# Attention score rows of 576 keys in one PSUM tile of two banks, a running minimum of negated scores, and small operations moved off VectorE

## The chip, the cores and the metric

The kernel runs on one core of a Trainium2 chip. Its engines are TensorE (PE in the profile; its weight loads are PEld), VectorE (DVE), ScalarE (ACT), GpSimd (POOL) and SyncE (SP), which issues most of the DMAs. A time is the device time of the whole program in microseconds (us); the lower the better. Before the change three runs took 1487.26, 1487.73 and 1488.32 us: median 1487.73.

## The reference

One transformer layer over a sequence of 2048 tokens of width 256, all in float32: differential attention, then a feed-forward block, each behind a layernorm, followed by a layernorm and a residual addition. Cut to what matters here:

```python
qkv = hidden @ Wqkv_w.T + Wqkv_b              # 16 query heads, 8 key heads of 128
s  = (q_m . k_m) * 128**-0.5, causal          # m = 0, 1: the two maps of a pair
p  = softmax(s_0) - lam * softmax(s_1)        # 8 pairs of heads in 4 groups
o  = p @ v                                    # v: 4 groups of width 256
o  = o * rsqrt(mean(o*o) + 1e-5) * subln_w * (1 - LAMBDA_INIT)
x  = x + layernorm(o @ out_w.T + out_b)
x  = x + layernorm(ffn(layernorm(x)))         # two Hadamard transforms, silu gate
```

`lam` comes from four small vectors. Every score row is divided by its own sum of exponentials, and the row's maximum is taken off before the exponential.

## The kernel before

**Units and steps.** The attention goes through 4 groups; a group has its 2 query pairs side by side, so 64 queries of both pairs fill the 128 partitions. A block of 128 tokens (`i` = 0 to 15) has two halves of 64 queries. For `i` < 8 one *unit* covers both halves, above that each half is a unit of its own: 24 units in a group, 96 in all. A half `s` of block `i` sees L = 128 i + 64 (s + 1) keys. Group 0 goes up through the blocks; groups 1 to 3 take the long ones first, downwards, then the short ones, downwards.

The order of every engine's instructions is written out by hand: a loop over steps calls the parts of several units in turn, and dictionaries (`before`, `mid`, `between`, `after`) put projections, weight loads and pieces of the feed-forward at given steps. Each engine runs its own instructions in that order; waits are set from the tiles that are read and written. In step s:

- `begin`, `scores(new, 0)`: score matmuls of the first half of the unit's score rows (each row once for each of the two maps m), into PSUM tiles of two banks (`sc`, pool `ps_s`, three buffers, which projections, transposes and the feed-forward use as well). [...] VectorE copies the scores into `e` and keeps a running maximum in `mx` (L270); the last 64 keys get the causal mask and end the maximum in `last` (L281). A small VectorE operation makes the bias `nb` = -SCALE x last (L293).
- `exponentials` (ScalarE, L298): Exp with bias `nb` and scale SCALE, in place, with the row's sum in `d`.
- `inverse` of the unit of step s - 4: VectorE forms `u` = ss/256 + ed (L395), GpSimd its power -0.5 `f` (L399), and GpSimd scales the unit's output rows `osb` by it (L401). `ss` is the sum of squares of the output row, `ed` = EPS x d x d.
- `turn_out` of the unit of step s - 5, where its block is complete: VectorE transposes `osb` into `xo` (L417), and SP writes it out and reads it back transposed (`oT`).
- `combine` of the unit of step s - 1 on VectorE: reciprocal of the second sum (L317), `cf` (L319), e0 + cf x e1 (L325), then 32x32 transposes (L347), a DMA to DRAM and four back (`pt`, by SP); last of all `ed` (L333).
- Then projections put there, `scores(new, 1)`, `values` of the unit of step s - 3 (TensorE into `po`; ScalarE copies it to `osb` and squares it with a sum into `ss`, L382 and L385), `project_out`, and `exponentials(new, 1)`.

**Cutting rows into tiles.** A row has up to 1024 columns in one tile. Rows of 576, 1088 and 1600 keys are cut by hand:

```python
if L % 512 == 64 and L > 64:
    first = 320 if L == 576 else 704
    return [first, L - first]
```

So a row of 576 keys takes two tiles, with 320 and 256 columns. There are two such rows (m = 0 and 1) in each group, both in the unit `i` = 4.

**Start.** The projections (L174) are evicted by ScalarE and VectorE with a bias column of `colv` (L192, L194); `colv` is loaded by a DMA of GpSimd. `load_lambdas` issues four more loads on GpSimd's queue, and 16 columns of `colv` hold the biases of the query heads. The last stage, from about 1310 us on, is the feed-forward alone; pieces of it already run beside the last units.

## Time and profile before

| | |
|---|---|
| median of three runs | 1487.73 us |
| profiled execution, its own time | 1489.19 us |
| its span | 1487.4 us |
| TensorE busy | 1458.2 us (98%) |
| VectorE busy | 1080.8 us (73%) |
| ScalarE busy | 498.6 us (34%) |
| GpSimd busy | 287.1 us (19%) |
| score matmuls (L260), 1280 records | 481.3 us |
| score scans (L270), two groups | 231.5 and 100.5 us |
| masked last scan (L281), 248 records | 70.4 us |

The profile is one execution, recorded by the hardware. Busy time is the time in which an engine has an instruction at work; matmuls overlap each other, so a busy TensorE is not one at its peak. A float32 matmul shows as two records (two passes). In lists of waits, "A <- B" means that A stood until B had ended. In lists of groups, the columns are line, engine, operation, output<-inputs, shapes, count | busy us, mean ns of one | idle time before it and what ended most of it. In a timeline the columns are start (us), duration (us), engine, line, operation, count, and in brackets the idle time before it. Line numbers are those of the kernel before.

### The profile page before, as it was taken

The numbers are of one execution on the slowest core, as the hardware profiler recorded it, in microseconds if no ns is written. First come the engines' busy times: TensorE is split into PE (matmuls) and PEld (weight loads), VectorE is DVE, ScalarE is ACT, GpSimd is POOL, SyncE is SP. The second block draws the span as 40 slices with busy tenths as digits, with TensorE's granted clock in tenths as the row PEclk, the third lists the DMA queues.
The fourth block names the chain that finished last, engine by engine and source line by source line (L and its number), as shares of the span: only waits on it lengthen the run. The fifth ranks groups of instructions, "written<-read, shape, count | busy, mean of one in ns | idle before, by whom it ended". The sixth has DMA issues, their size and how long they took to land.

```text
span 1487.4 us, 17643 instructions
## 1 busy us (share of the span) xinstructions
PE 1458.2 (98%) x5488; PEld 1040.3 (70%) x5488; DVE 1080.8 (73%) x2828; ACT 498.6 (34%) x1011; POOL 287.1 (19%) x379
## 2 busy tenths in 40 slices
PE   8899999999999999999999999999999999999998
PEld 5567777656766776665677776665776666888887
DVE  4489788847666889654878787547898888866674
ACT  2354334333123334322423334324223334541211
POOL 2022222101111121110321211112221221322110
PEclk9999999999999999999999999999999999999999
DMA  3049898866467787721898788424987768522000
GB/s 116 21 107 188 184 193 186 152 121 128 88 141 147 168 201 166 149 78 43 183 171 189 164 198 176 98 64 91 252 181 160 161 154 172 137 79 64 26 25 15
DMA packets 463838, 198.41 MB, mean 133 GB/s; under 512 B 366177, under 2 KB 460913, under 8 KB 463745
## 3 DMA queue, kind: packets, MB, share of 16 engines
q1 hardware_dynamic: 459616, 187.36, 58.8%
q0 software_dynamic: 2592, 8.48, 2.0%
q10 hardware_dynamic: 1536, 1.44, 0.3%
q8 instruction: 45, 0.74, 0.2%
q14 instruction: 49, 0.39, 0.1%
HBM read 104.95 MB, written 92.27 MB: 133 GB/s over the span
## 4 chain that ended last, share of the span: by engine, by line
PE 86%; DVE 11%; DMA 1%; issue 1%; ACT 1%; ACTq 0%; SPq 0%; POOL 0%; POOLq 0%; DVEq 0%
PE po L371 28%; PE sc L260 25%; PE pp L174 11%; PE gu L650 7%; PE pout L438 7%; PE pd L680 4%; PE pv L202 4%; DVE e L270 3%; DVE e L325 2%; DVE e L347 2%; DVE e L281 1%; DMA wq<-in_wqkvT 1%; DVE xo L417 0%; PE tx L637 0%; DVE nb L293 0%
## 5 line engine op out<-in xcount | busy, mean ns | idle before, releaser
L260 PE MATMUL sc<-k,q 128*128 128x512 f32 (+7 forms) x1280 | 481.3, 522 | 14.6 <-DVE last L281 8.9
L371 PE MATMUL po<-v,pt 128*128 128x256 f32 x2176 | 485.4, 379 | 0.0
L371 PEld LDWEIGHTS po<-v,pt 128*128 128x128 f32 x2176 | 425.3, 196 | 57.6 <-issue 10.2
L260 PEld LDWEIGHTS sc<-k,q 128*128 128x128 f32 x1280 | 236.7, 191 | 238.5 <-issue 188.3
L298 ACT ACTIVATE e<-e,nb 128x192 f32<-128x192 f32 (+28 forms) x256 | 299.4, 1170 | 296.9 <-DVE u L395 172.6
L270 DVE TENSOR_SCALAR_CACHE_REDUCE e<-sc 128x1024 f32<-128x1024 f32 (+14 forms) x248 | 231.5, 934 | 158.3 <-PE sc L260 157.7
L399 POOL TENSOR_TENSOR f<-u,mhalf 128x1 f32<-128x1 f32 (+1 forms) x96 | 59.5, 620 | 948.2 <-DVE u L395 644.6
L382 ACT COPY osb<-po 128x256 f32<-128x256 f32 (+1 forms) x96 | 42.7, 444 | 427.1 <-PE po L371 427.0
L174 PE MATMUL pp<-xnT,wq 128*128 128x512 f32 x384 | 173.7, 603 | 3.8 <-ACT xnT L498 2.4
L347 DVE STREAM_TRANSPOSE e<-e 128x768 f32<-128x768 f32 (+7 forms) x192 | 172.4, 938 | 6.7
L401 POOL TENSOR_SCALAR osb<-osb,f 128x256 f32<-128x256 f32 x128 | 172.3, 1351 | 9.5
L325 DVE SCALAR_TENSOR_TENSOR e<-e,cf,e 128x64 f32<-128x64 f32 (+31 forms) x128 | 170.6, 1353 | 3.4
L174 PEld LDWEIGHTS pp<-xnT,wq 128*128 128x128 f32 x384 | 73.4, 193 | 88.8 <-issue 80.5
L438 PE MATMUL pout<-wo,oT 128*128 128x256 f32 x512 | 120.9, 379 | 0.0
L270 DVE TENSOR_SCALAR_CACHE_REDUCE e<-sc,mx 128x192 f32<-128x192 f32 (+13 forms) x136 | 100.5, 739 | 23.6 <-PE sc L260 9.5
L438 PEld LDWEIGHTS pout<-wo,oT 128*128 128x128 f32 x512 | 97.3, 190 | 12.8
L281 DVE CUSTOM_DVE_ANT_0 e<-sc,mask,mx 128x64 f32<-128x64 f32 x248 | 70.4, 284 | 8.9
L663 ACT ACTIVATE hT<-gu,colv 128x256 f32<-128x256 f32 x64 | 30.4, 475 | 133.6 <-PE gu L650 89.6
L650 PE MATMUL gu<-fxnT,wgate 128*128 128x256 f32 x256 | 65.8, 379 | 0.2 <-DVE last L281 0.2
L650 PE MATMUL gu<-fxnT,wup 128*128 128x256 f32 x256 | 65.7, 379 | 0.0
L664 DVE SCALAR_TENSOR_TENSOR hT<-gu,colv,hT 128x256 f32<-128x256 f32 x64 | 30.9, 482 | 40.1 <-ACT hT L663 40.0
L202 PE MATMUL pv<-wq,xnT 128*128 128x256 f32 x256 | 57.6, 380 | 0.9 <-DVE xnT L499 0.8
(105 smaller groups left out, 942.6 us busy)
## 6 DMA issues: line engine op xcount, KB each, us to landing
dr<-e SPq DMA_DIRECT2D x20, 1024.0 KB, 4.7
pt<-dr SPq DMA_DIRECT2D x80, 256.0 KB, 5.8
dr<-e SPq DMA_DIRECT2D x20, 896.0 KB, 4.3
pt<-dr SPq DMA_DIRECT2D x80, 224.0 KB, 5.1
do<-xo SPq DMA_DIRECT2D x64, 256.0 KB, 3.0
oT<-do SPq DMA_DIRECT2D x256, 64.0 KB, 2.8
dr<-e SPq DMA_DIRECT2D x20, 768.0 KB, 4.0
pt<-dr SPq DMA_DIRECT2D x80, 192.0 KB, 4.5
```

The costliest lines, as they stand in the source:

```text
L174: nc.tensor.matmul(pp[:, ts(h, 512)], lhsT=wq[:, c, ts(j, P)], rhs=xnT[:, c, cols4], start=(c == 0), stop=(c == 1),)
L202: nc.tensor.matmul(pp[:, ts(t, 256)], lhsT=xnT[:, c, ts(nb * 4 + t, P)], rhs=wq[:, c, 768:1024], start=(c == 0), stop=(c == 1),)
L260: nc.tensor.matmul(sc[:, lo : lo + ww], lhsT=qT[m][:, u.i, u.subs[a]].rearrange("d p q -> d (p q)"), rhs=kT[m][:, at + lo : at + lo + ww], ...
L270: nc.vector.tensor_scalar(e[:, at : at + full], sc[:, :full], 1.0, best, ALU.mult, ALU.max, accum_out=u.mx[:, k0, c : c + 1],)
L281: nc.vector.tensor_tensor_reduce(e[:, L - 64 : L], sc[:, full : full + 64], mask, 1.0, best, ALU.add, ALU.max, accum_out=u.last[:, k0 : k0 ...
L298: nc.scalar.activation(e, e, AF.Exp, bias=u.nb[:, 2 * a + m : 2 * a + m + 1], scale=SCALE, accum_out=u.d[:, a, m : m + 1],)
L325: nc.vector.scalar_tensor_tensor(e0, e1, cf[:, a : a + 1], e0, ALU.mult, ALU.add)
L347: nc.vector.transpose(xv[:, r], ev[:, r])
L371: nc.tensor.matmul(u.po[:, ts(a, HID)], lhsT=ptv[:, g, r, :], rhs=vt[:, kc, :], start=(kc == 0), stop=(kc == u.i),)
L401: nc.gpsimd.tensor_scalar(u.osb[:, a, :], u.osb[:, a, :], f[:, a : a + 1], None, ALU.mult)
L438: nc.tensor.matmul(u.pout[:, :HID], lhsT=u.oT[:, c, p, :], rhs=wos[u.g][:, p, c, :], start=(p == 0 and c == 0), stop=(p == 1 and c == 1),)
L650: nc.tensor.matmul(ps[:, ts(2 * j + n, 256)], lhsT=ffn[which][:, c, ts(fc, P)], rhs=xnT[:, c, :], start=(c == 0), stop=(c == 1),)
```

## The change

Six edits, all in the attention:

1. A row of 576 keys takes one tile: 256 columns in its first bank, 320 in the second. One VectorE scan reads the 512 unmasked ones out of both banks, the masked one reads the 64 at column 768. Rows of 1088 and 1600 keys are cut as before.
2. The queries are projected as -SCALE x q: the evictions get a scale, and the 16 bias columns of the query heads are multiplied by -SCALE once, on GpSimd, ahead of the loads in `load_lambdas`. Scores are then negated and scaled, the running maximum becomes a running minimum, mask and start value change sign, and Exp takes `last` as its bias with scale -1. `nb` and its operation are gone.
3. `ed` is made by ScalarE (Square with a scale, 256 EPS d d) behind the Exps of the unit's second half, in place of VectorE at the end of `combine`.
4. `u` is an addition on GpSimd, ss + ed, in place of VectorE.
5. The factor 16 that is then missing in `f` is a second scalar in GpSimd's scaling of `osb`.
6. The query evictions of VectorE become a multiplication and an addition in one operation.

```diff
@@ project_heads
+                scale = -SCALE if j < 4 else 1.0
                 if h == 0 or not both:
-                    nc.scalar.activation(dst, src, AF.Identity, bias=bias)
+                    nc.scalar.activation(dst, src, AF.Identity, bias=bias, scale=scale)
                 else:
-                    nc.vector.tensor_scalar(dst, src, bias, None, ALU.add)
+                    nc.vector.tensor_scalar(dst, src, scale, bias, ALU.mult, ALU.add)
...
         def cuts(L):
 
-            if L % 512 == 64 and L > 64:
-                first = 320 if L == 576 else 704
-                return [first, L - first]
+            if L == 1088 or L == 1600:
+                return [704, L - 704]
             return [min(1024, L - c) for c in range(0, L, 1024)]
...
-            u.nb = sm.tile([P, 4], F32, tag="nb", name=f"nb_{u.n}")
...
-                best = LOWEST
+                best = HIGHEST
...
-                    for lo in range(0, w, 512):
-                        ww = min(512, w - lo)
+
+                    step = 256 if w == 576 else 512
+                    los = [0, 256] if w == 576 else range(0, w, 512)
+                    for k, lo in enumerate(los):
+                        ww = w - lo if k == len(los) - 1 else step
                         nc.tensor.matmul(
-                            sc[:, lo : lo + ww],
+                            sc[:, 512 * k : 512 * k + ww],
...
+                    tail = 768 if w == 576 else full
                     if full:
+                        dst, src = e[:, at : at + full], sc[:, :full]
+                        if w == 576:
+                            dst = dst.rearrange("p (k c) -> p k c", k=2)
+                            src = sc.rearrange("p (k c) -> p k c", k=2)[:, :, :256]
                         nc.vector.tensor_scalar(
-                            e[:, at : at + full],
-                            sc[:, :full],
+                            dst,
+                            src,
                             1.0,
                             best,
                             ALU.mult,
-                            ALU.max,
+                            ALU.min,
                             accum_out=u.mx[:, k0, c : c + 1],
                         )
...
-                            sc[:, full : full + 64],
+                            sc[:, tail : tail + 64],
                             mask,
                             1.0,
                             best,
                             ALU.add,
-                            ALU.max,
+                            ALU.min,
                             accum_out=u.last[:, k0 : k0 + 1],
                         )
                     at += w
-            lo, hi = (2 * half, 2 * half + 2) if u.ns == 2 else (half, half + 1)
-            nc.vector.tensor_scalar(u.nb[:, lo:hi], u.last[:, lo:hi], -SCALE, None, ALU.mult)
...
                     AF.Exp,
-                    bias=u.nb[:, 2 * a + m : 2 * a + m + 1],
-                    scale=SCALE,
+                    bias=u.last[:, 2 * a + m : 2 * a + m + 1],
+                    scale=-1.0,
                     accum_out=u.d[:, a, m : m + 1],
+                )
+            if half:
+
+                u.ed = sm.tile([P, 2], F32, tag="ed", name=f"ed_{u.n}", bufs=8)
+                nc.scalar.activation(
+                    u.ed[:, : u.ns], u.d[:, : u.ns, 0], AF.Square, scale=16.0 * math.sqrt(EPS)
                 )
@@ combine
-            u.ed = sm.tile([P, 2], F32, tag="ed", name=f"ed_{u.n}", bufs=8)
...
-            nc.vector.scalar_tensor_tensor(
-                u.ed[:, : u.ns], d1, EPS, d1, ALU.mult, ALU.mult
-            )
@@ inverse
-            nc.vector.scalar_tensor_tensor(
-                w[:, : u.ns], u.ss[:, : u.ns], 1.0 / 256.0, u.ed[:, : u.ns], ALU.mult, ALU.add
-            )
+            nc.gpsimd.tensor_tensor(w[:, : u.ns], u.ss[:, : u.ns], u.ed[:, : u.ns], ALU.add)
             nc.gpsimd.tensor_tensor(f[:, : u.ns], w[:, : u.ns], mhalf[:, : u.ns], ALU.pow)
             for a in range(u.ns):
                 nc.gpsimd.tensor_scalar(
-                    u.osb[:, a, :], u.osb[:, a, :], f[:, a : a + 1], None, ALU.mult
+                    u.osb[:, a, :], u.osb[:, a, :], f[:, a : a + 1], 16.0, ALU.mult, ALU.mult
                 )
@@ load_lambdas
+            nc.gpsimd.tensor_scalar(
+                colv[:, C_QKB : C_QKB + H], colv[:, C_QKB : C_QKB + H], -SCALE, None, ALU.mult
+            )
```

More of the change, by code (lines that the diff above doesn't have):

```diff
@@ L34 @@
 WARM = 12
-MASKED = -1e30
-LOWEST = -3e38
+MASKED = 1e30
+HIGHEST = 3e38
 C_QKB = 0
@@ L392, in inverse @@
         def inverse(u):
+            f = sm.tile([P, 2], F32, tag="f", name=f"f_{u.n}")
             w = sm.tile([P, 2], F32, tag="u", name=f"u_{u.n}")
-            nc.vector.scalar_tensor_tensor(
-                w[:, : u.ns], u.ss[:, : u.ns], 1.0 / 256.0, u.ed[:, : u.ns], ALU.mult, ALU.add
-            )
-            f = sm.tile([P, 2], F32, tag="f", name=f"f_{u.n}")
+            nc.gpsimd.tensor_tensor(w[:, : u.ns], u.ss[:, : u.ns], u.ed[:, : u.ns], ALU.add)
             nc.gpsimd.tensor_tensor(f[:, : u.ns], w[:, : u.ns], mhalf[:, : u.ns], ALU.pow)
```

## The prediction

> **What bounds the kernel now.** I read the engine shares first, then the chain of work that ended last, then PE's waits, and last the places where PE stood. From the page:
>
> ```profile
> PE 1458.2 (98%) x5488; PEld 1040.3 (70%) x5488; DVE 1080.8 (73%) x2828; ACT 498.6 (34%) x1011; POOL 287.1 (19%) x379
> ...
> PE 86%; DVE 11%; DMA 1%; issue 1%; ACT 1%; ACTq 0%; SPq 0%; POOL 0%; POOLq 0%; DVEq 0%
> ```
>
> PE is the bound, and the matmuls stay as they are, so a gain can only come out of PE's standing time. Next, what ended PE's waits (us in total, times, longest):
>
> ```profile
> PE sc L260 <- DVE last L281: 8.9, 9, 2.4
> PE pp L174 <- ACT xnT L498: 2.4, 1, 2.4
> PE sc L260 <- DVE e L270: 2.3, 5, 1.0
> ```
>
> L281 is the masked maximum, the last reader of a score tile: PE waits for a PSUM buffer that a late DVE still has to read. Full-speed pace is 0.216 us per pass of 256 columns (26 in the 5.61 us that the chain gives them) and 0.43 per 512. Read from the start of every matmul, time beyond that pace adds up to some 39 us; about 11 lie before 62 us (start-up; the change takes nothing there) and 2 after 1310 (feed-forward alone). One of the clearest places, in order of time (start, us, then what ended the idle time):
>
> ```profile
> 591.88 0.70 PE L260 MATMUL sc<-k,q 128*128 128x320 f32 x2
> ...
> 592.67 0.12 DVE L333 SCALAR_TENSOR_TENSOR ed<-d 128x2 f32<-128x2 f32 x1
> ...
> 593.85 0.08 DVE L281 DVE_READ_ACCUMULATOR2_ANT last<- 128x1 f32 x1
> 593.85 0.89 DVE L270 TENSOR_SCALAR_CACHE_REDUCE e<-sc 128x704 f32<-128x704 f32 x1
> ...
> 594.08 0.67 PE L260 MATMUL sc<-k,q 128*128 128x256 f32 x2 [1.50 <-DVE last L281]
> ...
> 594.99 0.08 DVE L281 DVE_READ_ACCUMULATOR2_ANT last<- 128x1 f32 x1
> 595.11 0.17 DVE L293 TENSOR_SCALAR nb<-last 128x2 f32<-128x2 f32 x1
> 595.18 0.48 DVE L270 TENSOR_SCALAR_CACHE_REDUCE e<-sc 128x320 f32<-128x320 f32 x1
> ...
> 595.22 1.21 PE L260 MATMUL sc<-k,q 128*128 128x320 f32 x4 [0.47 <-DVE last L281]
> ...
> 596.70 3.67 PE L174 MATMUL pp<-xnT,wq 128*128 128x512 f32 x8 [0.27 <-DVE last L281]
> ```
>
> These are the 576-key rows: two tiles per score row (320, then 256 columns), four in all, with three PSUM buffers. PE needs 2 x (0.54 + 0.43) = 1.94 us for them and takes 596.70 - 591.88 = 4.82: 2.9 lost. DVE ran without a wait for PE since 562.4, so it is late from a long backlog. The stretches (us, then busy time of PE, PEld, DVE, ACT, POOL; PEclk is the granted clock):
>
> ```profile
> 562.40:593.70 31.30, 30.18 (x111) 20.82 (x109) 29.87 (x77) 12.97 (x29) 5.49 (x9) 1.00 0.74 150
> 1122.60:1160.00 37.40, 36.23 (x131) 24.77 (x129) 35.78 (x77) 11.87 (x21) 6.03 (x8) 1.00 0.73 153
> 1192.80:1251.00 58.20, 54.08 (x196) 37.21 (x195) 53.97 (x159) 22.19 (x48) 11.86 (x18) 0.97 0.71 160
> 1246.80:1250.10 3.30, 3.08 (x6) 1.91 (x7) 1.85 (x11) 2.42 (x5) 0.00 (x0) 0.50 0.89 268
> ```
>
> In each of the first three DVE is busy for 93 to 96% of the time, and what is left are small gaps between its operations: it has work waiting throughout. The last is a half-clock stretch right after PE stood 2.4 us.
>
> [...]0.50 for 1246.8 to 1250.1, and 0.51 for 65.8 to 69.2, each behind a stand of about 2.4 us; none behind the 1.5 us one at 592. [...]the combine (L325) of 512 columns takes 912 ns on average, that of 576 only 858. [...]
>
> **The change part by part.** DVE durations from the groups by shape:
>
> ```profile
> L293 DVE TENSOR_SCALAR nb<-last 128x1 f32<-128x1 f32 x128 | 19.7, 154 | 4.5
> L395 DVE SCALAR_TENSOR_TENSOR u<-ss,ed 128x1 f32<-128x1 f32 x64 | 9.6, 150 | 0.0
> L333 DVE SCALAR_TENSOR_TENSOR ed<-d 128x1 f32<-128x1 f32 x64 | 7.5, 118 | 0.0
> L399 POOL TENSOR_TENSOR f<-u,mhalf 128x1 f32<-128x1 f32 x64 | 36.4, 569 | 606.0 <-DVE u L395 328.1 <-DVE r L317 277.9
> ```
>
> *Removed from DVE.* Operations overlap, so start to start counts. nb starts 0.12 after the accumulator read (594.99 to 595.11) and the next 0.07 later; without an nb the next scan starts together with that read (593.85, 593.85). So nb costs 0.19 (at least its 0.07), u 0.07, ed 0.04. Per unit: two nb, one u, one ed = 0.49; 96 units: 47 us of DVE, of which only what lies in a late stretch counts. Counted in the order of DVE's instructions, in 562.4 to 593.7 stand 5 nb, 3 u, 3 ed: 0.95 + 0.21 + 0.12 = 1.3 us. In 1122.6 to 1160: 6, 3, 3: 1.5. In 1192.8 to 1251: 10, 5, 5: 2.5.
>
> *576 keys.* 8 score rows in all. DVE: scans of 320 and 192 took 1.08 start to start; one of 512, between 619 (448 columns) and 750 (576), takes 0.69 + 0.13: 0.26 saved each. A scan over two banks is not in the trace; [...]I take 0. PE: same widths, but two tiles, so it writes a whole row and waits for one release per row; the next projection or row no longer waits for this row's own scans.
>
> *Added on ACT.* 96 Squares; the nearest row is the 128x2 ACTIVATE at L520, 202 ns; each waits for the Exp before it on its own engine, so 0.2 to 0.4 each, 19 to 38 us. ACT is 34% busy and idles 123 us for nb alone. Behind it stand the next Exp or eviction; without cover at PE's waits for ACT it costs at most 3 x 0.4 us. The Exp takes its bias from the minimum itself, and with two rows per unit no longer waits for the second: earlier by one scan.
>
> *Added on POOL.* 96 additions; between 0.09 (a small MEMSET) and the pow's 0.57 to 0.72; I take the pow's, 60 us. POOL now waits for ACT's ss instead of u behind DVE's scans: at 592.8 instead of 598.2 in the stretch shown, so f comes earlier despite the addition. Behind it stand the pad's memset, in the last group also residual loads and layernorm pows; they stood behind the same ss before. Its reader, the transpose at L417, has 0.0 idle; if osb were late, this would hold combine and its DMAs. The second scalar (16) at L401, the second one in the DVE evictions (747 ns) and the scale on ACT's: 0. Column scaling, once, at most 0.65: four load issues at 8.45 start later; lambdas landed 6.1 after issue, 14.6, read at 16.36, first q eviction at 19.20: 0. SP's order is unchanged.
>
> **The sum** (PE time lost now, and saved):
> - 63.2: PE waits for ACT's xnT copy behind Exps: 2.5 + 1.7 for the half clock; Exps earlier by 0.35 to 1: 0.6.
> - 85.3 (576 in group 0) 0.4: all. 101.9, 1.1: 0.3.
> - 592 and 910, 2.9 each: the row's second tile waits for the release at 594.08 - 1.3 = 592.8, and PE arrives at 592.85; the projection needs 595.22 - 1.3 = 593.9 and PE arrives at 593.8. 0.2 remains, 2.7 x 2 = 5.4.
> - 725 and 1044, 0.5 and 0.2: 0.5.
> - 1135 and 1158, 0.66 and 1.27: DVE's 1.5.
> - 1203 and 1225, 0.63 and 1.29: DVE has saved 0.5 and then 1.5: 1.5.
> - 1243 to 1250, 4.9: the stand of 2.5 keeps 2.5 - (2.3 - 1.5) = 1.7, and 0.2 at the second row; 1.3 saved beside the half clock, which costs 1.7 and, at 1.7 us of standing, is likelier gone: 1.2.
>
> 0.6 + 0.7 + 5.4 + 0.5 + 1.5 + 1.5 + 2.5 = 12.7 us. The profiled execution took 1489.19 (span 1487.4), the runs' median is 1487.73; I subtract from the median: **1475.0**.
>
> **Rivals.** *Only the tiles pay:* nb is worth its 0.07 and DVE's saving ends as DVE waiting for PE. Then at 592 and 910 the second row starts at 594.08, 1.23 after PE could, is done at 595.05, and the projection starts at 595.22: 2.9 - 1.23 - 0.17 = 1.5 saved each. With 0.4 at 85 and about half of the other DVE terms, some 2: 5.5 in all, about 1482. For it: the overlap of small operations; against: the 593.85 pair. *Clock:* the half clock stays at both places, or goes at both: 1.7 worse or 1.5 better; 1473 to 1477. *It doesn't do what it says:* ACT or POOL is the one that was late, and the gaps stay: within 0.2% of before, 1487; against: PE's waits name DVE last, and L417 never waited. *Slower:* the minimum scans run slower than the maximum ones. No row shows one. In the three stretches scans and maxima are about half of DVE's time (in the first 11.1 us of scans and 3.1 of maxima in 29.9); at +25% they add 3.5, 3.5, 3.9 and 6.5 us at 562, 880, 1122 and 1192 against savings of 1.3, 1.3, 1.5 and 2.5, so some +11 less 3 for the tiles: 1496. It decides from about +12%. Against: an addition over 1024 columns (L579) takes 1.22 us like the scan with maximum, so the operation doesn't set the pace.
>
> **How the numbers follow.** Main case, 1472 to 1479: 0.65, the clock cases in it. Only tiles, 1479 to 1484: 0.23. No change: 0.07. Slower: 0.05. A measurement of this kernel can tell about 0.2% (3 us) from no change. 1472 to 1482.5 holds 8 in 10. Faster 0.88, same 0.07, slower 0.05.
>
> **What would show it.** DVE near 1023 us busy (56 of small operations less, 2 of scans), PE's busy time unchanged, POOL near 347, ACT near 520. PE's waits that end with L281 fall from 8.9 us to about 3, and the ones at 592 and 910 vanish. Wrong if scans of 1024 columns leave 1.22 us, if L417's successor shows idle time for POOL, or if new PE waits for ACT appear.

## The result

The kernel after takes 1475.56 us (median of six runs, 1474.48 to 1477.58), the kernel before beside it 1487.85: a ratio of 0.9919, 95% interval 0.9906 to 0.9932, or 12.3 us less; predicted was 1475.0, between 1472 and 1482.5. A later measurement on another occasion gave 1475.05 and 0.9918 (0.9900 to 0.9935). The profiled execution of after took 1475.96 us with a span of 1474.2, against 1489.19 and 1487.4 before: 13.2 us less in the span.

In the kernel after the lines have moved: the score matmul is L262, the scan L277, the masked scan L288, Exp L303, `ed` L314, the combine L335, its transposes L354, `pt` L366, the sum of squares L392, `u` L403, `f` L404, the scaling of `osb` L406. The page of after, engine shares and chain of the work that ended last:

```profile
PE 1452.5 (99%) x5488; PEld 1040.0 (71%) x5488; DVE 1030.7 (70%) x2428; ACT 507.7 (34%) x1107; POOL 203.8 (14%) x476
...
PE 88%; DVE 8%; DMA 2%; issue 1%; ACT 1%; SPq 1%; ACTq 0%; POOL 0%; POOLq 0%; DVEq 0%
```

VectorE's share of the chain went from 11% to 8%, and PE's rose. But DMA rose from 1 to 2%, and GpSimd, which was given 96 additions, is busy for 83 us *less*. Both come up below. PE's waits of after (us in total, times, longest):

```profile
PE sc L262 <- DVE last L288: 3.3, 5, 1.3
...
PE pp L174 <- ACT xnT L503: 1.4, 1, 1.4
...
PE po L378 <- DMA pt<-dr: 1.0, 1, 1.0
```

The waits that end with the masked scan fell from 8.9 to 3.3 us, the one for ScalarE's `xnT` copy from 2.4 to 1.4, and a wait for a DMA is new. To see where the 13.2 us came from, I added up, for both profiled executions, what PE's matmuls took from start to start beyond their full-speed pace; in all this is 38.8 us before and 25.7 after, which accounts for all but 0.1 us of the difference of the spans. By place (times of the kernel before; us lost; "saving predicted" and "measured" are differences of these losses):

| place | before | after | saving predicted | measured |
|---|---|---|---|---|
| start-up, to 15 | 6.93 | 5.42 | 0 | 1.5 |
| 60 to 72, `xnT` copy | 5.39 | 3.39 | 0.6 | 2.0 |
| 85 and 102 | 1.57 | 0.45 | 0.7 | 1.1 |
| 592 | 2.95 | 1.15 | 2.7 | 1.8 |
| 910 | 2.97 | 1.16 | 2.7 | 1.8 |
| 725 and 1044 | 0.68 | 0 | 0.5 | 0.7 |
| 1056 of after, new | 0 | 1.28 | 0 | -1.3 |
| 1135 and 1158 | 1.93 | 0.77 | 1.5 | 1.2 |
| 1203 and 1225 | 1.90 | 0.27 | 1.5 | 1.6 |
| 1243 to 1250 | 4.84 | 2.07 | 2.5 | 2.8 |
| sum | | | 12.7 | 13.2 |

The total was met, but not line by line: the two places that were to pay most paid a third less, one new loss appeared, and the start and the place at 63 gave more. The experiments are about the first three of these; the start is taken up behind them. (A loss from start to start is some 0.16 us more than the idle time that a view puts in brackets for the same stand: the record of a pass of 256 columns lasts 379 ns on average in before's `values`, at a pace of 216, so records overlap.)

The place that answers to 592, in the timeline of after (start, us, then engine, line, operation; in brackets the idle time before it and what ended it):

```profile
587.15 1.13 PE L262 MATMUL sc<-k,q 128*128 128x256 f32 x4
...
587.68 0.86 DVE L277 TENSOR_SCALAR_CACHE_REDUCE e<-sc 128x704 f32<-128x704 f32 x1
...
588.80 0.08 DVE L288 DVE_READ_ACCUMULATOR2_ANT last<- 128x1 f32 x1
...
589.03 1.21 PE L262 MATMUL sc<-k,q 128*128 128x256 f32 x4 [0.74 <-DVE last L288]
...
589.94 0.68 DVE L277 TENSOR_SCALAR_CACHE_REDUCE e<-sc 128x512 f32<-128x512 f32 x1
...
590.17 3.67 PE L174 MATMUL pp<-xnT,wq 128*128 128x512 f32 x8
```

Four tiles (320 and 256 columns, twice) have become two rows of one tile each, 587.15 to 590.17, so 3.02 us against 4.82. The scan over two banks takes 0.68 us for 512 columns, so the assumption that it is no dearer held. But the second row still waits, although the prediction had it arrive just after its buffer came free.

### The profile page after: what moved, and what is told of

It reads as the page before. It is cut to its first block, busy times and chain, and to the rows that moved or that the text cites. A ratio compares the mean times of both kernels' runs of the same rounds, so it can differ in the third digit from the quotient of the medians.

```text
span 1474.2 us, 17392 instructions
## 1 busy us (share of the span) xinstructions
PE 1452.5 (99%) x5488; PEld 1040.0 (71%) x5488; DVE 1030.7 (70%) x2428; ACT 507.7 (34%) x1107; POOL 203.8 (14%) x476
## 4 chain that ended last, share of the span: by engine, by line
PE 88%; DVE 8%; DMA 2%; issue 1%; ACT 1%; SPq 1%; ACTq 0%; POOL 0%; POOLq 0%; DVEq 0%
PE po L378 28%; PE sc L262 26%; PE pp L174 11%; PE pout L443 7%; PE gu L658 7%; PE pd L688 4%; PE pv L203 4%; DVE e L277 2%; DVE e L335 1%; DVE e L354 1%; SPq L366 1%; DMA wq<-in_wqkvT 1%; DMA pt<-dr 1%; DVE e L288 1%; DVE xo L422 0%
## 5 line engine op out<-in xcount | busy, mean ns | idle before, releaser
L262 PE MATMUL sc<-k,q 128*128 128x512 f32 (+7 forms) x1280 | 478.8, 520 | 7.6 <-DVE last L288 3.3
L262 PEld LDWEIGHTS sc<-k,q 128*128 128x128 f32 x1280 | 236.6, 190 | 228.4 <-issue 185.3
L303 ACT ACTIVATE e<-e,last 128x192 f32<-128x192 f32 (+28 forms) x256 | 299.6, 1171 | 239.2 <-DVE last L288 216.6
L277 DVE TENSOR_SCALAR_CACHE_REDUCE e<-sc 128x1024 f32<-128x1024 f32 (+15 forms) x248 | 231.0, 932 | 190.7 <-PE sc L262 190.2
L354 DVE STREAM_TRANSPOSE e<-e 128x768 f32<-128x768 f32 (+7 forms) x192 | 172.3, 937 | 6.7
L174 PE MATMUL pp<-xnT,wq 128*128 128x512 f32 x384 | 170.6, 594 | 3.1 <-DMA wq<-in_wqkvT 1.4
L335 DVE SCALAR_TENSOR_TENSOR e<-e,cf,e 128x64 f32<-128x64 f32 (+31 forms) x128 | 166.2, 1319 | 3.4
L403 POOL TENSOR_TENSOR u<-ss,ed 128x1 f32<-128x1 f32 (+1 forms) x96 | 21.0, 218 | 945.4 <-ACT po L392 945.3
L277 DVE TENSOR_SCALAR_CACHE_REDUCE e<-sc,mx 128x320 f32<-128x320 f32 (+13 forms) x128 | 97.1, 759 | 21.6 <-PE sc L262 7.8
L288 DVE CUSTOM_DVE_ANT_0 e<-sc,mask,mx 128x64 f32<-128x64 f32 x248 | 70.4, 284 | 8.9
L406 POOL TENSOR_SCALAR osb<-osb,f 128x256 f32<-128x256 f32 x128 | 62.4, 487 | 12.3
L404 POOL TENSOR_TENSOR f<-u,mhalf 128x1 f32<-128x1 f32 (+1 forms) x96 | 60.8, 633 | 7.5
```

Source lines behind the costliest of these rows:

```text
L174: nc.tensor.matmul(pp[:, ts(h, 512)], lhsT=wq[:, c, ts(j, P)], rhs=xnT[:, c, cols4], start=(c == 0), stop=(c == 1),)
L262: nc.tensor.matmul(sc[:, 512 * k : 512 * k + ww], lhsT=qT[m][:, u.i, u.subs[a]].rearrange("d p q -> d (p q)"), rhs=kT[m][:, at + lo : at + ...
L277: nc.vector.tensor_scalar(dst, src, 1.0, best, ALU.mult, ALU.min, accum_out=u.mx[:, k0, c : c + 1],)
L288: nc.vector.tensor_tensor_reduce(e[:, L - 64 : L], sc[:, tail : tail + 64], mask, 1.0, best, ALU.add, ALU.min, accum_out=u.last[:, k0 : k0 ...
L303: nc.scalar.activation(e, e, AF.Exp, bias=u.last[:, 2 * a + m : 2 * a + m + 1], scale=-1.0, accum_out=u.d[:, a, m : m + 1],)
L335: nc.vector.scalar_tensor_tensor(e0, e1, cf[:, a : a + 1], e0, ALU.mult, ALU.add)
```

## Experiments

All times are medians; each ratio is to the kernel before, run beside it, with its 95% interval. "After" is 1475.56 or, on the second occasion, 1475.05.

### The tiles alone, and the tiles undone

The first kernel is before with the tile edit alone, the second is after without it:

```diff
 # tiles alone, on before; the scan still takes the maximum
-            if L % 512 == 64 and L > 64:
-                first = 320 if L == 576 else 704
-                return [first, L - first]
+            if L == 1088 or L == 1600:
+                return [704, L - 704]
...
 # tiles undone, on after
-            if L == 1088 or L == 1600:
-                return [704, L - 704]
+            if L % 512 == 64 and L > 64:
+                first = 320 if L == 576 else 704
+                return [first, L - first]
```

> The kernel before with the 576-key rows in one two-bank tile and nothing else (maximum, nb, u and ed stay where they were). Both theories give the tiles the same worth alone: at 592 and at 910 the second row starts at the release of 594.08 as before, is done at 595.05, and the projection starts at the release of 595.22 and not at 596.70: 1.5 us each, with 0.4 at 85: 3.4 us less than before, about 1484.4. If the tiles carry more than that (the prediction's 2.7 a place were tile, not DVE), 1482 or less; if the scan over two banks is dearer, its duration is over 0.69 us per 512 columns.

> The kernel after with the 576-key rows split again into tiles of 320 and 256. The sums of the two edits are independent if this costs what the tiles alone saved: 3.4 us, about 1479. If the two edits overlap (DVE now early enough to make the old tiles harmless), under 1.5 us, about 1477; if the tiles are what lets the DVE savings through, 5 us or more, 1480.5 and up.

Measured: tiles alone 1483.41, ratio 0.9969 (0.9957 to 0.9981), 4.1 us less than before; tiles undone 1479.99, ratio 0.9950 (0.9939 to 0.9962), 4.4 to 4.9 more than after. Both are a little over the 3.4 expected. The timeline of the kernel with the tiles alone, at the same place:

```profile
592.13 1.13 PE L261 MATMUL sc<-k,q 128*128 128x256 f32 x4
...
594.33 1.21 PE L261 MATMUL sc<-k,q 128*128 128x256 f32 x4 [1.06 <-DVE last L287]
...
595.47 1.52 PE L174 MATMUL pp<-xnT,wq 128*128 128x512 f32 x3
```

and of the kernel with the tiles undone:

```profile
588.40 0.70 PE L263 MATMUL sc<-k,q 128*128 128x320 f32 x2
590.27 0.67 PE L263 MATMUL sc<-k,q 128*128 128x256 f32 x2 [1.17 <-DVE last L289]
591.41 1.21 PE L263 MATMUL sc<-k,q 128*128 128x320 f32 x4 [0.47 <-DVE last L289]
592.70 0.67 PE L174 MATMUL pp<-xnT,wq 128*128 128x512 f32 x1
```

From the first score matmul to the projection: before 4.82, tiles alone 3.34, tiles undone 4.30, both edits 3.02. The tiles are worth 1.48 us here on before and 1.28 on after (predicted: 1.5, as the rival *only the tiles pay* had priced it), everything else together 0.3 to 0.5. The prediction had counted 1.2 for everything else. So the miss is nearly all in VectorE's gain, not in the tiles. The two edits hardly overlap: 4.1 us alone, 4.4 to 4.9 on top.

### VectorE's time of nb, without Exp's wait for it

Where had VectorE's gain gone? The prediction took it that VectorE "has work waiting throughout" from 562 to 594. In after's timeline of VectorE, over the same stretch, it has not:

```profile
568.51 0.96 DVE L277 TENSOR_SCALAR_CACHE_REDUCE e<-sc 128x768 f32<-128x768 f32 x1 [0.56 <-PE sc L262]
...
579.71 0.82 DVE L277 TENSOR_SCALAR_CACHE_REDUCE e<-sc 128x640 f32<-128x640 f32 x1 [0.73 <-PE sc L262]
```

Relieved of its small operations it catches up with PE twice and waits 0.56 + 0.73 = 1.29 us for scores. From its first scan of the stretch to the one at 592.71 VectorE took 30.23 us in before (from 562.48), and from 557.75 to 587.68, 29.93, in after: with the waits it does 1.6 us less work, but only 0.3 arrives. (The 1.6 are the predicted 1.3 and, for most of the rest, the one combine of 1024 columns there: 1.50 us before, 1.28 after.) What is saved after its last wait is one nb, one u and one ed, 0.3 us. To test this, nb is put back and read by nothing:

```diff
                     at += w
+            lo, hi = (2 * half, 2 * half + 2) if u.ns == 2 else (half, half + 1)
+            nc.vector.tensor_scalar(u.nb[:, lo:hi], u.last[:, lo:hi], -SCALE, None, ALU.mult)
```

> The kernel after with nb computed again on VectorE once per half, in its old place, but read by nothing: Exp still takes the minimum itself. This returns the VectorE time of 192 small operations and not the wait of Exp. Theory carry (the prediction): each nb in a late stretch comes off PE's standing at 0.19 us: 0.95 at each of 592 and 910, 1.1 at 1135 and 1158, 1.9 at 1203 to 1250, 1 elsewhere: about +6 us, 1481.5. Theory catch-up: in the kernel after, VectorE catches up with PE inside the stretch (it waits 0.56 us at 568.5 and 0.73 at 579.7), so before those moments a saving or a cost counts for nothing: 0.2 at each of 592 and 910, 0.9 at 1135 and 1158, 1.2 at 1203 to 1225, 1 elsewhere: about +3.5 us, 1479; and VectorE's two waits in that stretch shrink to less than half.

Measured: 1480.23, ratio 0.9945 (0.9933 to 0.9957), 4.7 to 5.2 more than after, between the two theories. Place by place it is clear, because PE's loss at 592 and at 910 grows from 1.15 to 1.34 each: 0.19, one nb, as catch-up says, and not 0.95. VectorE's two waits of that stretch, in this kernel:

```profile
568.33 0.96 DVE L278 TENSOR_SCALAR_CACHE_REDUCE e<-sc 128x768 f32<-128x768 f32 x1 [0.15 <-PE sc L263]
...
579.53 0.82 DVE L278 TENSOR_SCALAR_CACHE_REDUCE e<-sc 128x640 f32<-128x640 f32 x1 [0.32 <-PE sc L263]
```

They are 0.41 shorter each, that is two nb at 0.2, and two stand ahead of each: the slack pays for them, not PE. The other places, from 60 to 1243, lose some 3.4 us, between the 3.1 that catch-up and the 4.0 that carry had for them; they do not tell the two apart. That the median rises by more than the 3.8 us of the places is taken up with the clock below.

### u and ed back on VectorE

```diff
-                nc.scalar.activation(
-                    u.ed[:, : u.ns], u.d[:, : u.ns, 0], AF.Square, scale=16.0 * math.sqrt(EPS)
-                )
...
+            nc.vector.scalar_tensor_tensor(
+                u.ed[:, : u.ns], d1, 256.0 * EPS, d1, ALU.mult, ALU.mult
+            )
...
-            nc.gpsimd.tensor_tensor(w[:, : u.ns], u.ss[:, : u.ns], u.ed[:, : u.ns], ALU.add)
+            nc.vector.tensor_tensor(w[:, : u.ns], u.ss[:, : u.ns], u.ed[:, : u.ns], ALU.add)
```

> The kernel after with u and ed on VectorE again (two small operations per unit), all else as after. Theory carry: 0.11 us per unit in the late stretches: 0.33 at each of 592 and 910, 0.33 at 1135, 0.55 from 1203: +1.5 us, 1477. Theory catch-up: only the one after VectorE's last wait counts at 592 and 910: 0.1 each, and 0.3 and 0.4 later: +0.9, 1476.5. If GpSimd's path was the point (u waiting in VectorE's queue delays the scaling of the output), more than +3.

Measured: 1476.34, ratio 0.9928 (0.9916 to 0.9940), 0.8 to 1.3 more than after. That is the size that catch-up gives, but carry's 1.5 is too near to be told from it by the time. The places say catch-up: 592 and 910 rise by 0.13 each, not 0.33. In all the places lose 2.1 us, more than either theory had, since 102, which neither listed, loses 0.5, and those from 1203 to 1243 lose 1.0; and there is no wait at 1056, which gives 1.3 back. Why, comes up with the last experiment but one.

### GpSimd's scaling: form and neighbour

The prediction expected GpSimd's busy time to go up to 347 us, and it went down to 203.8. The reason is the scaling of the output tile, 128 times 256 columns (mean ns of one ahead of the last bar): 1351 before, 487 after. Two kernels separate the number of its scalars from the rest:

```diff
 # before, with a second scalar of 1.0
-                    u.osb[:, a, :], u.osb[:, a, :], f[:, a : a + 1], None, ALU.mult
+                    u.osb[:, a, :], u.osb[:, a, :], f[:, a : a + 1], 1.0, ALU.mult, ALU.mult
...
 # after, with one scalar; the factor sits in the scales of the two Squares
-                    u.osb[:, a, :], u.osb[:, a, :], f[:, a : a + 1], 16.0, ALU.mult, ALU.mult
+                    u.osb[:, a, :], u.osb[:, a, :], f[:, a : a + 1], None, ALU.mult
```

> The kernel before with one edit: GpSimd's scaling of the output tile takes a second scalar (1.0, multiply) in place of none. Theory form: the two-scalar form itself is the quick one, so the 128 scalings fall from 1351 ns on average to about 490 and GpSimd's busy time from 287 us to about 177. Theory contention: the long scaling was caused by what VectorE did beside it, and the form changes nothing: 1351 ns stay. For the time: GpSimd is off the path, so within 0.2% of before (1484.9 to 1490.8); if a shorter scaling frees VectorE's combines from contention, VectorE's combines fall by some 34 ns on average (4 us in all) and the time by 0.5 to 1.5 us.

> The kernel after with the scaling of the output in its old form of one scalar; the factor 16 goes into the scales of the two Squares on ScalarE instead. Theory form: the scalings return to about 1350 ns, GpSimd's busy time from 204 to about 310 us. The time: off the path, so within 1 us of after (1475 to 1477); if GpSimd's length is part of the gain, VectorE's combines rise by some 30 ns each and the time by 0.5 to 1.5 us.

Groups by shape of GpSimd, of after, then of the first of these kernels, then of the second:

```profile
L406 POOL TENSOR_SCALAR osb<-osb,f 128x256 f32<-128x256 f32 x128 | 62.4, 487 | 12.3
...
L403 POOL TENSOR_TENSOR u<-ss,ed 128x1 f32<-128x1 f32 x64 | 14.8, 231 | 612.3 <-ACT po L392 612.2
```

```profile
L401 POOL TENSOR_SCALAR osb<-osb,f 128x256 f32<-128x256 f32 x128 | 99.8, 786 | 9.5
```

```profile
L407 POOL TENSOR_SCALAR osb<-osb,f 128x256 f32<-128x256 f32 x128 | 120.2, 945 | 9.5
```

Both theories are half right. Record by record, an undisturbed scaling takes 0.93 us with one scalar and 0.48 with two: the form. And beside VectorE's combine many are stretched, up to 2.75 us: the neighbour. Before, 120 of the 128 overlap a combine, because `u` stood in VectorE's queue just ahead of one, and 51 of these, and no other, are over 5% longer than undisturbed; after, GpSimd starts when ScalarE's sum is done, and 4 of 128 meet a combine. The combine pays as well: 1353 ns on average before, 1319 after, and 1354 again with `u` back on VectorE, where the two-scalar scaling takes 956. A shorter scaling does not spare it: with two scalars on before it takes 1371, where a fall of 34 was one of the expectations. The 912 ns that the prediction gives for the combine of 512 columns are the mean of three of 965 to 968 beside a scaling and one of 748 with GpSimd idle; the four of 1024 columns took 1500 to 1502 beside one in before and 1277 to 1280 without in after. (Three of the four of 576 columns took 819 ns beside one too, as without in after; the fourth 973.)

In the time neither shows. The first takes 1488.25, ratio 1.0000 (0.9991 to 1.0009); the second 1474.91, ratio 0.9911 (0.9896 to 0.9926), not to be told from after. GpSimd's 83 us are no part of the gain. But the first is not the same inside: it has a wait of 1.0 us for `pt` near 1066, which before has not, and its mean granted clock is higher. Both come up below.

### Exp waits for nb again

At 63 PE stands while ScalarE's `xnT` copy waits behind Exps. This kernel is the one with nb unread, but Exp reads it:

```diff
+            nc.vector.tensor_scalar(u.nb[:, lo:hi], u.last[:, lo:hi], 1.0, None, ALU.mult)
...
-                    bias=u.last[:, 2 * a + m : 2 * a + m + 1],
+                    bias=u.nb[:, 2 * a + m : 2 * a + m + 1],
```

> The kernel after with nb back in full: VectorE copies the minimum into nb once per half (factor 1.0), and Exp takes its bias from nb. Against the run with nb unread, which came to 1480.2, it adds only Exp's later start. Theory wait: at 63 the stand of PE before the projection goes from 1.7 back to 2.5 us (ScalarE's copy stands behind Exps that start later), and the half clock follows it in most executions: 0.8 plus 1.5 us, about 1482.5, mean granted clock 0.997 to 0.998. Theory chance: the half clock at 63 has nothing to do with the length of the stand: 0.8 alone, 1481, clock 0.999. Theory nothing: Exp has time to spare at every place: 1480.

Measured: 1481.21, ratio 0.9956 (0.9942 to 0.9970): 1.0 more than with nb unread by the medians and 1.6 by the ratios, where the theory of the wait had 2.3 and that of chance 0.8; the intervals overlap, so the time does not decide. In the profile the stand went from 1.72 to 2.53 us as expected, and the half clock followed; the mean clock of the five executions is 0.9978, against 0.9986 with nb unread. The windows of this kernel around it (stretch, length, then busy time of PE, PEld, DVE, ACT, POOL; then the granted clock):

```profile
60.40:63.80 3.40, 1.35 (x10) 0.88 (x8) 3.08 (x17) 2.59 (x10) 0.00 (x0) 1.00 0.00 0
63.80:67.20 3.40, 3.08 (x4) 1.51 (x5) 1.13 (x3) 0.27 (x1) 0.15 (x1) 0.50 0.24 80
```

The kernel before with two scalars had the same stand of 2.53 us at the same place, and no half clock after it; it had one at 594.7 instead, behind a stand of 1.66 that the prediction had called too short for it:

```profile
591.30:594.70 3.40, 1.44 (x5) 0.59 (x5) 3.29 (x12) 0.90 (x4) 0.00 (x0) 1.00 1.18 275
594.70:598.10 3.40, 3.40 (x7) 1.73 (x7) 2.78 (x17) 2.32 (x5) 0.47 (x1) 0.50 0.82 225
62.20:65.60 3.40, 2.11 (x12) 1.24 (x11) 3.13 (x20) 1.73 (x7) 0.00 (x0) 1.00 0.00 0
```

The trace's clock records show more. Within one execution all changes lie on one grid of 3.413 us: 11.13, 14.54, 65.74, 69.15, 1246.75 and 1250.17 in before are whole multiples of it apart, and each of the three stretches at half clock there is recorded with 3.413 us. From one execution to the next the grid is shifted: its first change is at 4.30 in before and at 5.24 in after. Call a piece of it from one point to the next a window. In before the windows that began at 7.71, 62.33 and 1243.34, with PE busy for 0.48, 0.34 and 0.28 of the time, were followed by one at half clock, and those at 591.39 and 908.83, with 0.54 and 0.59, were not. In the views above the window from 60.40 has 1.35 of 3.40, or 0.40, and the one from 591.30 has 0.42; both were followed, the one from 62.20, with 0.62, was not. Counted over the 13 profiled executions, from the clock's first rise to the last 10 us, every window in which PE was busy for less than 0.52 of the time was followed by one at half clock, none with more than 0.57 was, and between the two it went either way. (In the last 10 us two windows of 0.50 were not followed by one; why stays open.) That the share of a window decides is read from these counts; no run varied it by itself. Moving the grid over the profiled execution, I get the share of positions in which a stand leaves a window under 0.52:

| | 63 | 592 | 910 | 1243 | sum |
|---|---|---|---|---|---|
| before | 0.72 | 0.41 | 0.41 | 0.81 | 2.35 |
| tiles alone | 0.71 | 0 | 0 | 0.71 | 1.42 |
| nb unread | 0.32 | 0 | 0 | 0.59 | 0.91 |
| after | 0.20 | 0 | 0 | 0 | 0.20 |

This is an estimate, and the start is not in it, but it can be held against the runs. The mean granted clock over an execution is 0.9961 in 47 of before and 0.9990 in 11 of after; one stretch at half clock takes 3.41 x 0.5 / 1487 = 0.00115 off it, so before has 2.5 stretches more than after, against 2.15 in the table. With the tiles alone it is 0.9971, 0.9 stretches fewer than before, as in the table. Before with two scalars does not fit: its stands leave the same shares as those of before, yet its clock is 0.9972 over 13 executions, one stretch fewer; why stays open. A stretch costs 1.5 us at 63 (5.39 or 5.29 us lost with it, 3.84 without, at the same stand), 1.2 at 592 (4.12 and 2.95) and 1.0 at 1243 (4.84 and 3.83). For 2.5 stretches that makes some 3 us of the 12.3. A second way gives nearly the same: among the executions with a mean clock of 0.998, three of each kernel, the medians are 1485.38 and 1476.48, 8.9 apart, so 3.4 of the 12.3 go with the clock.

A longer stand at 63 by itself cost next to nothing: with nb unread PE stood 1.72 us and lost 3.77 in all from 60 to 72, in before with two scalars it stood 2.53 and lost 3.84, both without a half clock, because a wait a few matmuls later (0.71 in the former) was gone in the latter.

### The weights of the feed-forward, one step later

After's new wait: `values` at 1056 needs `pt`. The queue of SP in after issues the four transfers of `pt` in 13.83 us, against 3.97 for the ones that stand there in before:

```profile
1039.05 13.83 SPq L366 DMA_DIRECT2D pt<-dr  x4
```

```profile
1048.18 3.97 SPq L359 DMA_DIRECT2D pt<-dr  x4
```

GpSimd's part of after's timeline just ahead of it:

```profile
1037.91 0.79 POOL L543 DMA_DIRECT2D wup<-in_wupT  x1 [3.45 <-DVE v L210]
1038.69 0.73 POOL L544 DMA_DIRECT2D wgate<-in_wgateT  x1
1039.42 0.92 POOL L545 DMA_DIRECT2D wdown<-in_wdownT  x1
```

In before these loads (3.3 MB with a small one) come at 1054.43, after the transfers; the two slow scalings and the wait for `u` held GpSimd until then. One line moves them:

```diff
-        put(after, first + 3, load_ffn)
+        put(after, first + 4, load_ffn)
```

> The kernel after with the loads of the feed-forward weights (3.3 MB by GpSimd's queue) one step later in the program, all else as after. Theory collision: the new wait at 1056 is there because GpSimd, no longer held by VectorE, issues these loads at 1037.9, 1.1 us ahead of the four transfers that bring the turned exponentials back (their issue then takes 13 us and not 3 to 4). With the loads a step later these transfers issue in under 5 us, the wait at 1056 is gone, 1.0 to 1.3 us less than after, about 1474.2; VectorE's first use of the weights may then wait, which costs nothing unless PE's wait at 1100 grows beyond 0.54. Theory schedule: PE simply arrives earlier at the same transfers; then the wait at 1056 stays at about 1 us.

Measured: 1474.09, ratio 0.9906 (0.9891 to 0.9922), 1.0 to 1.5 less than after, as expected, though the interval overlaps that of after. The wait at 1056 is gone from the trace, which decides between the two theories. Two lines of SP's queue in this kernel:

```profile
1040.42 4.76 SPq L366 DMA_DIRECT2D pt<-dr  x4
...
1053.50 12.29 SPq L366 DMA_DIRECT2D pt<-dr  x4
```

The collision has not gone: the loads now meet the next `pt` (they start at 1052.81), but that one has time to spare, and PE loses nothing. In the kernel with `u` on VectorE the loads come at 1044.7, behind the `pt` issued from 1039.3 to 1043.8, which is why it had no wait there. The cause of the new wait is thus GpSimd running ahead. Moving `u` is one way to it (after with one scalar has the wait too), and the shorter scaling by itself another: in before with two scalars, where `u` is still on VectorE, the loads come at 1052.65, not behind the issue of `pt` (1048.96 to 1053.54) but in it, and PE waits 1.0 us for `pt`. That its time is no worse than that of before may be due to the one stretch of half clock that it has less.

### The combine's factor on GpSimd, and a kernel that beats both

`cf` and its reciprocal cost VectorE 0.41 us per unit. They went to GpSimd, behind the second Exp:

```diff
-            nc.vector.reciprocal(r2[:, : u.ns], d2)
-            nc.vector.scalar_tensor_tensor(
-                cf[:, : u.ns], d1, nlam, r2[:, : u.ns], ALU.mult, ALU.mult
-            )
...
+            nc.gpsimd.tensor_tensor(r2[:, : u.ns], d2, mone[:, : u.ns], ALU.pow)
+            nc.gpsimd.tensor_scalar(
+                u.cf[:, : u.ns], r2[:, : u.ns], nlam, 1.0, ALU.mult, ALU.mult
+            )
+            nc.gpsimd.tensor_tensor(u.cf[:, : u.ns], u.cf[:, : u.ns], d1, ALU.mult)
```

> The kernel after with the combine's factor (a reciprocal of 0.15 us and a product of 0.26, start to start, 96 of each on VectorE) computed on GpSimd right behind the second Exp: a power of -1 and two products, some 1 us, all early enough if VectorE is late. Theory carry: 0.41 us per unit in the late stretches: three units at 592 and at 910, three at 1135, five from 1203: about 1.2 each, 5 us in all, 1470.5. Theory catch-up: only the unit after VectorE's last wait counts at 592 and 910: 0.4 each, 0.8 at 1135 and 1158 (what is left there), 1 later: 2.5 us, 1473. If GpSimd's factor comes late, VectorE waits at the combine for it and the time rises above 1476.

Measured: 1474.09, ratio 0.9902 (0.9886 to 0.9918), 1.0 to 1.5 less than after: less than either theory, and its interval overlaps that of after. At 592 and 910 it brought 0.53 each and 0.6 at 1236, and the wait at 1056 (1.28) is gone, as the loads come at 1053.66 here. But VectorE now waits for GpSimd where rows are short, and near 1271 PE loses 0.9 more:

```profile
DVE e L342 <- POOL cf L329: 17.8, 17, 3.3
```

So the last kernel does this for rows of 768 keys and more only, and takes two more places: a key block in two PSUM tiles, and a transpose ahead of the Exps. Its core, on after:

```diff
+            pps = [
+                ps_s.tile([P, 1024], F32, tag="sc", name=f"pp_{g}_{nb}_{j2}_{h}")
+                for h in range(1 + split)
+            ]
...
-                        pp[:, ts(h, 512)],
+                        pps[h if split else 0][:, ts(h, 512)],
...
-                put_block(before, [end], g, 0, [2])
+                put_block(before, [end], g, 0, [2], split=True)
...
-        put(mid, 2, turn_in, 3)
+        put(before, 2, turn_in, 3)
...
+                if new.L[0] >= 768:
+                    ratio(new)
```

Here `ratio` is the GpSimd form above, and shorter rows keep VectorE's.

> The kernel after with three edits at the places where PE still stands: the combine's factor on GpSimd for rows of 768 keys and more only; the last key block of groups 1 and 2 projected into two PSUM tiles, one per head, so that the first head is evicted while PE does the second; the last transpose of the input ahead of the Exps of its step. If each does its part: 0.5 at each of 588 and 904, 0.4 at 1150 and 0.6 at 1233 (factor), 0.8 at each of 678 and 994 (key block), 1 to 1.5 at 60 (transpose): 5 us less than after, about 1470.5. If the ring of three PSUM buffers is too short for a projection in two tiles, the 0.8 stay; if the transpose comes before its input is normalised, PE stands at 50 to 60 instead: 1473.

> The kernel after, unchanged, on the same chip and beside the same runs as the two others of this call: 1474.5 to 1476.5, and a second look at it. If its lack of half-clock stretches belongs to it, its mean granted clock is 0.998 to 1.0 here too and no stretch at half clock stands near 63 or near 1236; if it was luck in one execution, they come back.

Measured: 1469.13, ratio 0.9873 (0.9858 to 0.9888), and after, beside it on the same chip, 1475.05, ratio 0.9918 (0.9900 to 0.9935). The intervals do not meet: 5.9 us less than after. Its first wait:

```profile
PE sc L267 <- DVE last L293: 1.6, 5, 0.7
```

By places: 0.53 at each of 592 and 910, the full 1.05 at each of 684 and 1002 (with one head per tile the first is evicted while PE does the second), 1.2 at 60, 0.45 at 1158, 0.6 at 1243, and 1.28 at 1056, as its loads come at 1050.0 and miss that `pt`. With the transpose early, the stand at 63 is 1.12 and not 1.53 us, and no position of the grid leaves a window under 0.52. The three edits were not run one by one; that each does its part is read from the places. In its second profile, too, after has no half clock between 4.3 us and its last microseconds; but over its five executions here the mean clock goes from 0.997 to 1.0, the lowest just under what was expected, so some still have such stretches.

## Why the prediction held, and where it failed

**Bound and cause: right.** PE is the bound, and where the change saved most, PE had stood for score tiles that VectorE released late. The waits that end with the masked scan were to fall from 8.9 to about 3; they are at 3.3.

**576 keys: right.** A row waits for one release; this saves 1.3 to 1.5 us at 592 and at 910, and 0.4 at 85. The two-bank scan is not dearer: 0.68 us for 512 columns, where 0.69 was taken.

**The sum at 592 and 910: wrong, by 0.9 each.** The failing step is "the row's second tile waits for the release at 594.08 - 1.3". It rested on the reading that VectorE has work waiting throughout, which holds at before's lateness only. In after VectorE has caught up with PE at 568.5, and again at 579.7; what arrives at 592 is 0.3. The waits there did not vanish; 1.15 remain. The rival *only the tiles pay* had this mechanism ("DVE's saving ends as DVE waiting for PE") and its 1.5 per place; it was wrong in the 0.07 per nb and in halving the other terms. In the stretches that end at 1135, 1203 and 1243 VectorE hardly waits for PE in after; between 1135 and 1158 it does, 0.61 us at 1138.5. There 1.2 + 1.6 + 2.8 came against 1.5 + 1.5 + 2.5.

**The worth of nb, u and ed: right.** 0.19 per nb is what the run with nb unread shows at 592, and 0.13 for one u and one ed, against 0.11, the run with these two back. For the total, 47 us start to start plus 2 of scans was the right measure (1080.8 to 1030.7: 50.1); the durations, on which the sign "DVE near 1023" rested, added up to 58, because small operations overlap.

**The clock: half clock behind stands right, sizes and places not.** A stretch was priced at 1.7 and costs 1.0 to 1.5. It was taken to follow a stand of 2.4 us and no shorter one, and credited at 1243 alone; in before with two scalars one followed a stand of 1.66 at 592. By the estimate its chance falls at 63, at 592, at 910 and at 1243, 2.35 to 0.20 in sum: about 3 us where 1.2 were counted.

**The start: put at 0, and wrong.** The prediction noted that the four loads at 8.45 start later, by at most the 0.65 us of the scaling of the bias columns, and counted only what waits for these loads. In after the scaling itself waits until `colv` has landed, and they start 2.75 later. The first line is of before, the others are of after:

```profile
8.45 0.61 POOL L504 DMA_DIRECT2D lt<-in_lams  x1
```

```profile
10.87 0.27 POOL L509 TENSOR_SCALAR colv<-colv 128x16 f32<-128x16 f32 x1 [2.74 <-DMA colv<-in_cols]
11.20 0.63 POOL L512 DMA_DIRECT2D lt<-in_lams  x1
```

What they leave free was not asked. The projection weights `wq` were issued long before them and are still on their way: the last of their four transfers lands at 17.1 to 18.1 us in the three profiles with the old start, and at 13.2 to 15.3 in the ten with the new one. The first value matmul then starts at 25.2 to 26.0 with the old start and at 22.7 to 25.0 with the new one. A half-clock stretch stands in the start as well (11.1 to 14.5 in before): in all three of the old, in five of the ten new. Beside these five alone, 24.4 to 25.0, the old start is 1.0 us later on average. So the 1.5 of the table is mostly such a stretch in this one pair of profiles; over all thirteen the new start is worth some 1.0 us beside the clock. That the later loads are the reason is read from the order of events, since no run moves them alone; whether the change also makes the stretch rarer stays open.

**Exps earlier at 63: 0.6 predicted.** They shortened the stand by 1.0 us; the time without the clock fell by 0.45 (3.84 to 3.39).

**GpSimd: wrong in three more ways that cost little.** The addition takes 0.22 us, not the pow's 0.57 to 0.72; the second scalar, put at 0, was in fact a gain of 0.45 us on each scaling; and GpSimd being done earlier, noted as harmless, moved 3 MB of loads ahead of `pt`: 1.3 us in the new wait. The prediction listed who stands behind GpSimd's instructions, residual loads and pows, and left out the weights of the feed-forward, and asked only what a later GpSimd would hold up.

**ScalarE: right on the path.** The Squares take 0.19 us each (0.2 to 0.4 expected), its busy time is 507.7 us and not 520, and no wait of PE for ScalarE grew. Of the other signs of being wrong none came: scans of 1024 columns take 1.21 us, and the transpose behind L417's place, L422 in after, does not wait for GpSimd.

The miss of 1.8 at 592 and 910, 0.3 at 1135 and 1.3 at 1056 was met by 1.5 at start-up, 1.4 at 63 and about 1 elsewhere. That the total came out within 0.6 us is luck to this extent: misses of 3.4 one way and 3.9 the other nearly cancelled.

## What to carry to other kernels

Time saved on an engine that runs late counts from the last moment at which it would catch up: subtract the saving from its lateness step by step along the stretch, and drop what exceeds it (here 0.3 of 1.6 us arrived at 592). An engine that is freed can act earlier, and so can the transfers that it issues (here at 1037.9 us and not at 1054.4); look for what these then meet, and, where transfers start later, for what is still on its way and may land sooner (here `wq`, by 15.3 us at the latest, with the old start by 17.1 at the earliest). Where stands of some 1.5 to 2.5 us were removed, compare the clock over many executions (here 0.9961 and 0.9990) before the gain is put down to the waits alone.

## What the hardware showed that was not expected

- GpSimd's multiplication of 128x256 by a column took 0.93 us with one scalar and 0.48 with two; beside VectorE's combine up to 2.75.
- The granted clock changed on a grid of 3.413 us only, shifted from one execution to the next. In before it halved behind windows with PE busy for 0.28, 0.34 and 0.48 of the time and not behind those with 0.54 and 0.59; over the 13 profiled executions it did so behind all below 0.52, but for two at the very end, and behind none above 0.57. A stretch cost 1.0 to 1.5 us.
- With four loads of GpSimd's queue (1 MB) issued 2.6 to 4.0 us later at the start, the weights in flight had landed by 13.2 to 15.3 us and not by 17.1 to 18.1.
- Four transfers of `pt` took 3.97 us to issue on SP's queue, and 13.83 where 3.3 MB of loads had been issued 1.1 us ahead of them on GpSimd's.
